# Four-layer convolution chain: the coarse wavelet sums of layer 1 as float32 products in 32-column strips

## The chip, the core and the metric

The kernel runs on one core of a Trainium2 chip. The metric is device time in microseconds (us) for one execution of the whole program, lower is better. Five engines work side by side and meet at semaphores: TensorE (PE in the profile, its weight loads PEld), VectorE (DVE), ScalarE (ACT), GpSimd (POOL) and SyncE (SP), whose queue issues the DMAs.

## The reference, cut to what matters

Four layers in a row work on `x` of 32 x 96 x 56 x 56 (batch, channels, rows, columns), each as `x = x + layer(_gn(x))`, where `_gn` is a normalisation over groups of three channels. Layer 0 is an expanding block with a depthwise convolution, layer 2 a quantised one, layer 3 a depthwise 9 x 9 convolution. The change is in layer 1, a wavelet convolution over three levels, for each channel by itself:

```python
def haar2d(x):
    a = x[:, :, 0::2, 0::2]; b = x[:, :, 0::2, 1::2]
    c = x[:, :, 1::2, 0::2]; d = x[:, :, 1::2, 1::2]
    ll = (a + b + c + d) * 0.5
    lh = (a - b + c - d) * 0.5
    hl = (a + b - c - d) * 0.5
    hh = (a - b - c + d) * 0.5
    return jnp.stack([ll, lh, hl, hh], axis=2)

cur = x
for i in range(3):
    co = haar2d(cur)
    cur = co[:, :, 0]                       # the sums go on to the next level
    flat = dwconv(co.reshape(B, C * 4, h, w), wconv_w[i]) * wscale[i]    # 5 x 5, depthwise
    level_coeffs.append(flat.reshape(B, C, 4, h, w))
next_ll = zeros
for i in reversed(range(3)):
    next_ll = ihaar2d(level_coeffs[i].at[:, :, 0].add(next_ll))
return dwconv(x, base_w) * base_scale + base_b + next_ll
```

So the first level works on 56 x 56, the second on the 28 x 28 sums of two by two points, the third on the 14 x 14 sums of those. What comes back from the third is added into the second, and that into the first.

## The kernel before

**Layout.** An image row of 56 is split into four column phases of 14 (`NPH`, `W4`). A channel's image is held in two halves `h` of 28 rows. One half lies in a tile with 112 partitions (28 rows x 4 phases) and 16 more for the halo of neighbouring rows, and 14 x 32 = 448 columns (column group, batch). Convolutions over rows and phases are then matrix products over the partitions, and steps between column groups are shifted views of the columns.

**Layer 1.** It goes over 48 pairs of channels. `load(i)` issues a pair's DMAs on SP: `images` (X, L736 and L739), `factors` (nr, L782), `matrices` (the row matrices of the first level, raw, L765 to L767; those of the second level, raw2, L838) and `third` (T3, L844). The steps are:

- `normal`: DVE scales and shifts X into x (L872, L873).
- `high` and `low`: ACT rounds x to float32r, a form that TensorE takes in one pass, into xh (L880); DVE writes the rest, x - xh, into xl (L884).
- `matrices1`, `matrices2`: ACT reorders raw and raw2 into T and T2 (L748, L775).
- `lowest1` (L897): the sums for the second level. Eight float32r products, for each half h, each parity n of the column group, and each of xh and xl, add up in one PSUM tile. Each (h, n) has its own 28 of the 112 output rows, and the other weights are zero. ACT copies the result to x2 (L900).
- `lowest2` (L906): the sums for the third level, two float32 products from x2; ACT copies them to x3 (L908).
- `level3` (L914), `level2` (L923, L924): the convolutions of the third and second level. ACT copies the third's output to c3 (L915, L916). The second's output is split into a rounded part and a rest, c2 (ACT L929, DVE L930).
- `level1`: `coarse` (L941) brings the second level up by float32r products, `fine` (L935) adds the first level by three float32 products, DVE adds the image (L954), and SP stores y (L961).

**Order.** PE, DVE, ACT and SP follow the program's order in this layer (`manual_schedule`). In one turn of the loop, pair i is in level1, pair i + 1 (`nxt`) in the sums and the upper levels, pair i + 2 (`far`) in normal and the matrices, and pair i + 3 is loaded. The turn begins with `load(i + 3)` and then:

```python
            do(lowest1, nxt)
            do(normal, far, 0, 0)
            do(matrices1, far, 0)
            do(normal, far, 0, 1)
            do(level1, i, 0, 0)
            do(lowest2, nxt)
```

Between the pairs, `left` gives out the last stores of layer 0 (L201), and `behind` prepares layer 2: its weights, and, every eighth pair, the first images that it will read (L1124). T2, T3, c2 and c3 are in three fixed sets of tiles, which POOL clears once at the start of the layer (L821). The first pair is prepared by `begin`.

**Names in the profile.** Numbers are left out of the names: the PSUM tiles pa1 and pa2 stand as pa, pc1 to pc3 as pc, x2 and x3 as x, T2 and T3 as T, c2 and c3 as c, raw2 as raw, y0 and y1 as y. In Layer 0, L426 is the expansion (full width), L449 and L493 are products that write strips of 32 columns, four of them next to each other.

Of the kernel before, what the change touches and what calls it, by code (L numbers as in the profile page):

```python
# [28 lines left out]
NPH = 4  # L29
# [599 lines left out]
NK = 3  # L629
# [128 lines left out]
LOW = 96  # L758

# [27 lines left out]
def layer1(ctx, tc, w, y0, left, made, norm, t1, t2, t3, y1, k2, behind):  # L787
# [18 lines left out]
    def rounded(name, shape):  # L806

        t = cp.tile(shape, F32R, tag=f"{name}r", name=f"{name}r")
        nc.scalar.copy(t, constant(name, shape))
        return t  # L810
# [3 lines left out]
    for i in reversed(range(NF)):  # L814
        sets[i] = {
            name: cp.tile(shape, dtype, tag=f"{name}{i}", name=f"{name}{i}") for name, shape, dtype in (
                ("T3", [128, 64 * KW], F32), ("T2", [PH, 2, NK, 128], F32), ("c2", [128, 2, 2, N2, B], F32R),
                ("c3", [128, N3, B], F32))}
# [4 lines left out]
    def load(i):  # L823

        st = {"i": i, **sets[i % NF], "X": [], "T": [None] * 2, "nr": [], "raw": [], "raw2": [], "pf": {}}
# [9 lines left out]
        def matrices(c):  # L835
            st["raw"].append(load_matrices(nc, pool, t1, c))
            raw = pool.tile([PH, NK * PH], F32, tag="raw2", name="raw2", bufs=4)
            nc.sync.dma_start(raw, t2[c])  # L838
            st["raw2"].append(raw)

        def third(c):
            at, n = c % 2 * HH, HH * KW
            for tile in range(2):
                nc.sync.dma_start(st["T3"][64 * tile + at : 64 * tile + at + HH, at * KW : at * KW + n], t3[c])  # L844
# [19 lines left out]
    def normal(st, j, h):  # L864

        if j + h == 0:
            st["x"] = pool.tile([128, 2, 2, W4, B], F32, tag="x", name="x", bufs=3)
            for n in ("xh", "xl"):
                st[n] = pool.tile([128, 2, 2, W4, B], F32R, tag=n, name=n, bufs=1)
# [5 lines left out]
    def parts(st, j):  # L875
        return (st[n][:, j].rearrange("p h q b -> p (h q b)") for n in ("x", "xh", "xl"))

    def high(st, j):
        x, xh, _ = parts(st, j)
        nc.scalar.copy(xh, x)  # L880

    def low(st, j):
        x, xh, xl = parts(st, j)
        nc.vector.tensor_tensor(xl, x, xh, ALU.subtract)  # L884

# [3 lines left out]
    def matrices2(st, j):  # L889
        ordered(nc, st["T2"][:, j], st["raw2"][j], 64)  # L890

    def lowest1(st):

        ps = psum.tile([128, 2, N2, B], F32, tag="w", name="pa1")
        parts = [(h, n, x) for h in range(2) for n in range(2) for x in ("xh", "xl")]
        for h, n, x in parts:
            nc.tensor.matmul(ps, low1[:, h, n, :], st[x][:, :, h, n::2, :],  # L897
                             start=((h, n, x) == parts[0]), stop=((h, n, x) == parts[-1]))
        st["x2"] = pool.tile([PH, 2, N2, B], F32, tag="x2", name="x2", bufs=2)
        nc.scalar.copy(st["x2"], ps[:PH])  # L900

    def lowest2(st):

        ps = psum.tile([128, N3, B], F32, tag="w", name="pa2")
        for j in range(2):
            nc.tensor.matmul(ps, low2[:, j, :], st["x2"][:, j], start=(j == 0), stop=(j == 1))  # L906
# [59 lines left out]
    def begin(st):  # L966
# [7 lines left out]
        for j in range(2):  # L974
# [4 lines left out]
            high(st, j)  # L979
        for j in range(2):  # L980
            low(st, j)
# [7 lines left out]
    with tc.manual_schedule(engines=MANUAL_SP):  # L989
        low1 = rounded("low1", [128, 2, 2, 128])  # L990
        up1 = rounded("up1", [128, 2, 2, 128])
        low2 = constant("low2", [PH, 2, 128])
        up2 = constant("up2", [128, 2, 128])
        pick = constant("pick", [C, 2, 128])
        for i in range(-3, PAIRS):
# [12 lines left out]
            do(high, far, 0)  # L1008
            do(low, far, 0)
# [6 lines left out]
            do(high, far, 1)  # L1016
# [4 lines left out]
            do(low, far, 1)  # L1021
# [551 lines left out]
def lowest_bands():  # L1573
# [24 lines left out]
    def twice(v, axis):  # L1598
        v = np.pad(v, [(0, 8 * (a == axis)) for a in range(v.ndim)])
        return np.concatenate([v, v], axis=axis)  # L1600

    return {"low1": low1, "low2": twice(low2, 2), "up1": up1, "up2": twice(up2, 0)}
# [115 lines left out]
```

## Time and profile before

| | us |
|---|---|
| median of 3 runs | 5655.76 (5650.31 to 5659.83) |
| the profiled execution | 5647.33 |
| its span, first to last instruction | 5645.5 |
| PE busy in the span | 5420.9 (96%) |
| DVE busy | 4691.7 (83%) |
| ACT busy | 4179.3 (74%) |
| POOL busy | 240.3 (4%) |

The 16 DMA engines together moved 456.13 MB in the span. The profile's page puts the span in 40 slices of 141 us; layer 1 lies in slices 20 to 25. A row of a group of instructions gives line, engine, operation, output and inputs, the form (weights' rows * columns, then partitions x columns), the count and the times. A row of the timeline gives start, length, engine, line and form; rows of the same kind that follow each other are merged, with their count at the end, and what is in brackets is the idle time before and what ended it. The end of a matmul is modelled and takes in the way through the array, so how often matmuls start tells what they cost.

### The profile page before, as it was taken

How to read it: one execution, taken by the hardware profiler on the slowest of the kernel's cores; microseconds unless marked ns; L12 is line 12 of the kernel's file. 1: busy time of each engine (PE TensorE's matmuls, PEld its weight loads, DVE VectorE, ACT ScalarE, POOL GpSimd, SP SyncE). 2: the span in 40 equal slices, each digit the busy share in tenths (PEclk: the TensorE clock that was granted, in tenths of full speed). 3: DMA queues.
4: the chain of work that ended last, by engine and by line, in shares of the span. 5: the costliest groups of instructions: out<-in, count | busy, mean ns of one | idle time of the engine just before them, and what ended most of it. 6: DMA issues, size and time to landing. Idle time of an engine off the chain costs nothing.

```text
span 5645.5 us, 137543 instructions
## 1 busy us (share of the span) xinstructions
PE 5420.9 (96%) x59704; PEld 3086.1 (55%) x59704; DVE 4691.7 (83%) x5413; ACT 4179.3 (74%) x6072; POOL 240.3 (4%) x161
## 2 busy tenths in 40 slices
PE   5999999999999999998899999999999999999999
PEld 2333333333333333333666666788878777787444
DVE  6999999999999999997777776777777777676777
ACT  5888888888888888885666664777777777676455
POOL 6000000000000000000000000000000000000000
PEclk9999999999999999998999999999999999999999
DMA  3023333322233232214577776479688697763888
GB/s 100 15 56 64 58 59 56 59 46 52 54 60 62 55 56 53 49 32 38 151 156 160 160 161 128 21 51 54 44 53 46 49 53 41 49 51 41 240 249 249
DMA packets 1289849, 456.13 MB, mean 81 GB/s; under 512 B 1104211, under 2 KB 1285187, under 8 KB 1287323
## 3 DMA queue, kind: packets, MB, share of 16 engines
q1 hardware_dynamic: 1289243, 447.32, 51.1%
q8 instruction: 469, 7.68, 0.6%
q14 instruction: 137, 1.12, 0.1%
HBM read 285.41 MB, written 214.08 MB: 88 GB/s over the span
## 4 chain that ended last, share of the span: by engine, by line
PE 82%; ACT 5%; DVE 5%; DMA 4%; issue 2%; SPq 1%; POOL 1%; ACTq 0%; DVEq 0%; POOLq 0%
PE psd L493 18%; PE psd L1294 13%; PE psj L548 11%; PE ps L426 8%; PE ps L1275 7%; PE pse L449 6%; PE pc L935 5%; PE pc L1469 4%; PE psj L1337 4%; DMA X<-y 2%; ACT hi L1245 2%; PE pc L923 1%; PE pa L897 1%; ACT u L1265 1%; DVE xl L884 1%
## 5 line engine op out<-in xcount | busy, mean ns | idle before, releaser
L467 DVE SCALAR_TENSOR_TENSOR h<-hpad,l_wdw,h 128x3136 f32<-128x3136 f32 x512 | 1782.2, 3481 | 9.1
L493 PE MATMUL psd<-plane,filt 128*32 128x392 f32 (+5 forms) x16384 | 1084.1, 485 | 0.6 <-issue 0.6
L1294 PE MATMUL psd<-apad,diag 64*64 64x392 bf16 x20736 | 914.5, 330 | 54.0 <-issue 50.1
L1294 PEld LDWEIGHTS <-diag 64*64 64x64 bf16 x20736 | 700.9, 106 | 262.8 <-issue 97.0
L493 PEld LDWEIGHTS psd<-plane,filt 128*32 128x32 f32 (+1 forms) x16384 | 389.5, 108 | 676.3 <-issue 623.5
L1265 ACT ACTIVATE u<-ps,o,s 128x784 int16<-128x784 f32 x576 | 537.4, 1003 | 164.9 <-PE ps L1275 145.9
L1265 ACT ACTIVATE a<-psd,o,s 128x784 int16<-128x784 f32 x448 | 424.6, 1002 | 263.3 <-PE psd L1294 263.2
L748 ACT COPY T<-raw 128x112 f32<-128x112 f32 (+2 forms) x1386 | 445.9, 385 | 230.0 <-DMA raw<-tdiff 170.3
L426 PE MATMUL ps<-xn,l_wboth 96*128 96x392 f32 (+1 forms) x1536 | 465.9, 506 | 23.9 <-ACT xn L408 23.2
L467 DVE SCALAR_TENSOR_TENSOR hc<-hhalf,l_wdw,hc 128x1568 f32<-128x1568 f32 x256 | 473.7, 1850 | 16.2 <-ACT hc L460 9.5
L1275 PE MATMUL ps<-hi,l_w1q 96*128 96x392 f32 x1280 | 464.0, 363 | 6.7 <-DVE u L1263 3.8
L935 PE MATMUL pc<-x,T 128*112 128x416 f32 (+1 forms) x1152 | 451.6, 529 | 6.1 <-DVE x L873 6.1
L1275 PE MATMUL ps<-lo,l_w1q 96*128 96x392 f32 x1280 | 439.2, 343 | 2.9 <-DVE lo L1253 2.9
L1469 PE MATMUL pc<-x,T 128*112 128x416 f32 (+1 forms) x1152 | 417.1, 523 | 13.8 <-ACT T L748 7.7
L449 PE MATMUL pse<-xn,l_wboth 96*32 96x392 f32 x4096 | 392.3, 501 | 4.5 <-ACT hab L470 4.5
L426 PEld LDWEIGHTS ps<-xn,l_wboth 96*128 96x128 f32 (+1 forms) x1536 | 219.4, 173 | 249.2 <-issue 54.5
L470 ACT ACTIVATE hab<-psd,o,s 128x784 f32<-128x784 f32 x256 | 283.7, 1113 | 59.5 <-PE psd L493 57.3
L1469 PEld LDWEIGHTS pc<-x,T 128*112 128x112 f32 x1152 | 203.2, 177 | 227.2 <-issue 188.7
L436 ACT ACTIVATE hpad<-ps,o,s 128x784 f32<-128x784 f32 x256 | 278.5, 1104 | 50.1 <-PE ps L426 48.8
L548 PE MATMUL psj<-h,wg 128*32 128x392 f32 x3072 | 306.4, 514 | 0.1
L548 PE MATMUL psj<-hab,wg 128*32 128x392 f32 x3072 | 304.8, 510 | 0.0
L935 PEld LDWEIGHTS pc<-x,T 128*112 128x112 f32 x1152 | 193.6, 180 | 154.9 <-issue 154.9
(267 smaller groups left out, 7684.8 us busy)
## 6 DMA issues: line engine op xcount, KB each, us to landing
X<-y SPq DMA_DIRECT2D x192, 392.0 KB
y<-xt SPq DMA_DIRECT2D x108, 392.0 KB
y<-y SPq DMA_DIRECT2D x96, 392.0 KB
out_dram<-y SPq DMA_DIRECT2D x96, 392.0 KB
twav<-zwav SPq DMA_DIRECT2D x768, 36.8 KB
y<-kept SPq DMA_DIRECT2D x72, 392.0 KB
xt<-y SPq DMA_DIRECT2D x59, 392.0 KB
xt<-in_x_dram SPq DMA_DIRECT2D x8, 2352.0 KB
```

The lines of the kernel that those rows point to most:

```text
L426: nc.tensor.matmul(ps[p, j, :NT], wexp[:, k * 128 : k * 128 + 128][:, m], im["xn"][:, j, rows, :].rearrange("c h w -> c (h w)"), start=Tru ...
L449: nc.tensor.matmul(ps[f * GC : (f + 1) * GC, half, :NT].rearrange("p (r w) -> p r w", w=W2), wexp[:, c : c + GC], im["xn"][:, f % 2, r0 : ...
L467: nc.vector.scalar_tensor_tensor(h2, taken(im, k, t), wdw[:, k, t : t + 1], h2, ALU.mult, ALU.add)
L470: nc.scalar.activation(view, ps, AF.Silu, bias=bi[1][:, c : c + 1], scale=sc[1][:, c : c + 1], accum_out=accum)
L493: nc.tensor.matmul(ps[at * GC : (at + 1) * GC, r, :NT].rearrange("p (r w) -> p r w", w=W2)[:, r0 - half * n : r1 - half * n, q0:q1], filt[ ...
L548: nc.tensor.matmul(ps[s * GC : (s + 1) * GC, t, :NT].rearrange("c (m r q) -> c r q m", m=2, q=W4), wg[p, k, c * GC : (c + 1) * GC], phases ...
L748: nc.scalar.copy(to.rearrange("x t (p s) -> x t p s", p=NPH), v[:, k])
L935: nc.tensor.matmul(ps[:PH, to], st["T"][j][:, h, k, :], st["x"][:, j, h, of], start=first and n == 0, stop=not first and n == NK - 1)
L1265: nc.scalar.activation(out, ps, AF.Identity, bias=o[:, c : c + 1], scale=s[:, c : c + 1])
L1275: nc.tensor.matmul(ps[:, j, :NT], w1[:, k * 128 : k * 128 + 128], im[part][:, r0 : r0 + RT, :].rearrange("c h w -> c (h w)"), start=(part ...
L1294: nc.tensor.matmul(ps[q, j, :NT].rearrange("p (r w) -> p r w", w=W), diag[p, k, t, :], v, start=(t == 0), stop=(t == 8))
L1469: nc.tensor.matmul(ps[:, :, to], st["T"][:, h, k, :], st["x"][:, h, :, of], start=(n == 0), stop=(n == NK - 1))
```

## The change

`lowest1` no longer reads high and low parts. Each (h, n) becomes one float32 product of x itself with a weight of 32 columns, 28 of them used, and writes its own strip of 32 PSUM partitions; nothing is added up. `high`, `low`, xh and xl go. x2 then has 128 partitions in four strips of 28 + 4. `lowest2` likewise makes four float32 products into four strips, two channels twice over, from one weight low2 of 128 x 32. To fit x2's partitions, T2 and raw2 are laid out in strips as well: raw2 becomes part of the fixed sets, is cleared by POOL, and is loaded by four DMAs for each pair of channels, in the second channel's turn, instead of one DMA for each channel. T3's blocks lie 32 instead of 28 apart. The constants low1, low2, up1 and up2 are built to match on the host.

```diff
+GC = 32
-                ("T3", [128, 64 * KW], F32), ("T2", [PH, 2, NK, 128], F32), ("c2", [128, 2, 2, N2, B], F32R),
+                ("T3", [128, 64 * KW], F32), ("T2", [128, 2, NK, 128], F32), ("raw2", [128, 2, NK * PH], F32), ("c2", [128, 2, 2, N2, B], F32R),
...
         def matrices(c):
             st["raw"].append(load_matrices(nc, pool, t1, c))
-            raw = pool.tile([PH, NK * PH], F32, tag="raw2", name="raw2", bufs=4)
-            nc.sync.dma_start(raw, t2[c])
-            st["raw2"].append(raw)
+            if c % 2:
+                for s in range(NPH):
+                    nc.sync.dma_start(st["raw2"][s * GC : s * GC + HH],
+                                      t2[c - 1 : c + 1, s * HH : (s + 1) * HH].rearrange("c x y -> x c y"))
 
         def third(c):
-            at, n = c % 2 * HH, HH * KW
+            at, n = c % 2 * GC, HH * KW
...
-    def high(st, j):
-        x, xh, _ = parts(st, j)
-        nc.scalar.copy(xh, x)
-
-    def low(st, j):
-        x, xh, xl = parts(st, j)
-        nc.vector.tensor_tensor(xl, x, xh, ALU.subtract)
...
     def matrices2(st, j):
-        ordered(nc, st["T2"][:, j], st["raw2"][j], 64)
+        ordered(nc, st["T2"][:, j], st["raw2"][:, j], 64)
 
     def lowest1(st):
 
         ps = psum.tile([128, 2, N2, B], F32, tag="w", name="pa1")
-        parts = [(h, n, x) for h in range(2) for n in range(2) for x in ("xh", "xl")]
-        for h, n, x in parts:
-            nc.tensor.matmul(ps, low1[:, h, n, :], st[x][:, :, h, n::2, :],
-                             start=((h, n, x) == parts[0]), stop=((h, n, x) == parts[-1]))
-        st["x2"] = pool.tile([PH, 2, N2, B], F32, tag="x2", name="x2", bufs=2)
-        nc.scalar.copy(st["x2"], ps[:PH])
+        for h in range(2):
+            for n in range(2):
+                strip = slice((2 * h + n) * GC, (2 * h + n + 1) * GC)
+                nc.tensor.matmul(ps[strip], low1[:, h, n, :], st["x"][:, :, h, n::2, :], start=True, stop=True)
+        st["x2"] = pool.tile([128, 2, N2, B], F32, tag="x2", name="x2", bufs=2)
+        nc.scalar.copy(st["x2"], ps)
 
     def lowest2(st):
 
         ps = psum.tile([128, N3, B], F32, tag="w", name="pa2")
-        for j in range(2):
-            nc.tensor.matmul(ps, low2[:, j, :], st["x2"][:, j], start=(j == 0), stop=(j == 1))
+        for strip in range(NPH):
+            nc.tensor.matmul(ps[strip * GC : (strip + 1) * GC], low2, st["x2"][:, strip % 2], start=True, stop=True)
...
-        low1 = rounded("low1", [128, 2, 2, 128])
+        low1 = constant("low1", [128, 2, 2, GC])
-        low2 = constant("low2", [PH, 2, 128])
+        low2 = constant("low2", [128, GC])
...
-            do(high, far, 0)
-            do(low, far, 0)
...
-            do(high, far, 1)
...
-            do(low, far, 1)
```

More of the change, by code (lines that the diff above doesn't have):

```diff
@@ L823, in load @@
     def load(i):
-        st = {"i": i, **sets[i % NF], "X": [], "T": [None] * 2, "nr": [], "raw": [], "raw2": [], "pf": {}}
+        st = {"i": i, **sets[i % NF], "X": [], "T": [None] * 2, "nr": [], "raw": [], "pf": {}}
         def images(c):
@@ L867, in normal @@
             st["x"] = pool.tile([128, 2, 2, W4, B], F32, tag="x", name="x", bufs=3)
-            for n in ("xh", "xl"):
-                st[n] = pool.tile([128, 2, 2, W4, B], F32R, tag=n, name=n, bufs=1)
         v, X, nr = st["x"][:, j, h], st["X"][j], st["nr"][j]
@@ L873, in normal @@
         nc.vector.tensor_tensor(v, v, bias, ALU.add)
-    def parts(st, j):
-        return (st[n][:, j].rearrange("p h q b -> p (h q b)") for n in ("x", "xh", "xl"))
-    def high(st, j):
-        x, xh, _ = parts(st, j)
-        nc.scalar.copy(xh, x)
-    def low(st, j):
-        x, xh, xl = parts(st, j)
-        nc.vector.tensor_tensor(xl, x, xh, ALU.subtract)
     def matrices1(st, j):
@@ L978, in begin @@
                 fine(st, j, h, True)
-            high(st, j)
-        for j in range(2):
-            low(st, j)
     sts = {}
@@ L1596, in lowest_bands, with strips @@
         up2[:, :, 64 * i : 64 * i + n] = low2[n * i : n * i + n].transpose(2, 1, 0)
[L1598 to L1602, printed above, removed]
+    def strips(v, axis):
+        shape = v.shape[:axis] + (-1, HH) + v.shape[axis + 1 :]
+        v = np.pad(v.reshape(shape), [(0, 4 * (a == axis + 1)) for a in range(v.ndim + 1)])
+        return v.reshape(v.shape[:axis] + (-1,) + v.shape[axis + 2 :])
+    of = [[low1[:, h, n, HH * (2 * h + n) : HH * (2 * h + n + 1)] for n in range(2)] for h in range(2)]
+    low1 = strips(np.array(of).transpose(2, 0, 1, 3), 3)
+    up2 = strips(up2, 0)
+    return {"low1": low1, "low2": strips(strips(low2[:, 0, :HH], 0), 1), "up1": up1, "up2": np.concatenate([up2, up2])}
 def layouts(a):
```

## The prediction

> **What bounds the kernel now.** I read the page first, then the windows of the second layer, then the waits there, then the order of time inside one pair of channels.
>
> ```profile
> span 5645.5 us, 137543 instructions
> PE 5420.9 (96%) x59704; PEld 3086.1 (55%) x59704; DVE 4691.7 (83%) x5413; ACT 4179.3 (74%) x6072; POOL 240.3 (4%) x161
> ```
>
> TensorE is busy nearly throughout, but a busy PE here may be waiting inside a modelled matmul, so the stage decides. Layer 1 runs from about 2677 to 3525 us, as 48 pairs of channels. The windows (busy time of PE, PEld, DVE, ACT, POOL, then granted clock, DMA share, GB/s), the last row one undisturbed pair:
>
> ```profile
> 3200.00:3300.00 100.00, 98.63 (x423) 66.57 (x423) 72.38 (x108) 65.25 (x182) 0.00 (x0) 1.00 0.72 146
> 3223.40:3239.93 16.53, 16.32 (x73) 11.07 (x71) 12.27 (x19) 10.85 (x31) 0.00 (x0) 1.00 0.58 162
> ```
>
> PE sets the pair's length; DVE has 4.3 us and ACT 5.7 us to spare. From the starts of the first sum product (L897) I get the 48 periods: about three quarters are 16.53 us within 0.02, the others are longer by 36 us together. Now one clean pair in order of time:
>
> ```profile
> 3239.65 1.09 DVE L884 TENSOR_TENSOR xl<-x,xh 128x896 fp32r<-128x896 f32 x1
> 3239.90 0.69 PE L897 MATMUL pa<-xh,low1r 128*128 128x448 f32 x1
> 3240.80 0.48 PE L897 MATMUL pa<-xl,low1r 128*128 128x448 f32 x1 [0.21 <-DVE xl L884]
> ...
> 3242.15 0.37 PE L897 MATMUL pa<-xl,low1r 128*128 128x448 f32 x1
> 3242.36 0.38 PE L941 MATMUL pc<-c,up1r 128*128 128x224 f32 x2
> 3242.57 2.31 PE L935 MATMUL pc<-x,T 128*112 128x448 f32 x6
> 3244.72 0.92 PE L906 MATMUL pa<-x,low 112*128 112x224 f32 x4
> 3245.32 0.54 PE L941 MATMUL pc<-c,up1r 128*128 128x224 f32 x2
> 3245.70 2.31 PE L935 MATMUL pc<-x,T 128*112 128x448 f32 x6
> 3247.93 1.24 PE L914 MATMUL pc<-x,T 64*64 64x224 f32 x10
> ```
>
> Starts count, not durations. Six records of L935 take 2.15 us (3242.57 to 3244.72). One float32 product is two records here (192 records of L906 are 96 products): 448 columns stream in 0.375 us a record, 224 columns in 0.187. A rounded product is one record: the L897 starts lie 0.207 apart. The first L897 starts about 0.33 before the L935 ahead of it is through (same offset at every pair), so the array is free for the sums at 3240.23 and goes on to L941 at 3242.36: **the first sum costs 2.13 us a pair**. Of that 8 x 0.207 = 1.66 is products and 0.47 is the wait for xl, which DVE finishes only at 3240.74. The second sum (L906) costs 4 x 0.187 and a little, 0.77.
>
> **The change, part by part.**
>
> *First sum.* Eight rounded products become four float32 ones, each into its own 32 columns. Nothing in Layer 1 is of that form, but Layer 0 has it:
>
> ```profile
> 907.08 1.52 PE L449 MATMUL pse<-xn,l_wboth 96*32 96x392 f32 x16
> 908.42 0.84 PE L493 MATMUL psd<-plane,filt 128*32 128x392 f32 x8
> ```
>
> Sixteen records of 392 columns, each 0.327 of streaming, take 1.34 us to the next line: not 5.2. They start in four waves of four, 7 ns apart in a wave, 0.309 to 0.333 between waves. L449 issues its strips one after another with one product each, as the change does, and L493 does so with 128 rows. So here: two waves of 0.375, plus 0.02 for the starts.
>
> Here a rule speaks against the change. The Trainium skill's page "FP8 and Floating Point Precision", section "TensorE Precision Notes", says true float32 takes four passes through the array. The trace agrees on the price of one product: 2 x 0.375 = 0.75 against 0.207 rounded. Taken alone it makes the sum 4 x 0.75 = 3.0 us, 0.9 dearer than now; by L449's row the four share one price, 0.77. I take the row, since it shows form and order both.
>
> Going in and out of strips costs something. "TensorEngine Tiling (Array Packing)", "Key Properties", says that a change of tiling mode drains TensorE, without a figure. The trace has one: L935 to the 64-column L914 takes 2.23 (3245.70 to 3247.93) against 2.15 to L906; the records give 93 ns there, 93 from L914 back to L941, and 95 from Layer 0's L426 into the strips of L449 and from them back. If the drain were a whole matmul's tail (an L449 record lasts 0.492 where it streams 0.327, so 0.165), the four switches of a pair would cost 0.28 more, 13 us in all; I take 0.095 and keep the other for the range.
>
> First sum after: 0.095 + 0.375 + 0.02 + 0.375 + 0.095 = 0.96. Saved: 2.13 - 0.96 = **1.17 us**. The xl wait goes with it, since x was written in the pair before. What is late next: the following L941 needs the c parts of DVE L930; they end 0.3 us before the sums now (3239.62), those of the half that is used first some 2 us earlier, so nothing waits even with the sum shorter.
>
> *Second sum.* 0.77 becomes 0.095 + 0.187 + 0.02 + 0.187 + 0.095 = 0.585; saved **0.18**. It needs ACT's copy x2, which ends 0.9 us after the sum while L941 and L935 run 2.4.
>
> *high and low.* Two ACT casts of 0.94 and two DVE subtractions of 1.09 leave each pair. DVE and ACT are not the bound, so beyond the xl wait they count nothing; DVE has about 10.1 and ACT 9.0 us of work in the new 15.2.
>
> *Same prices.* x2's copy writes 128 instead of 112 partitions, T2's copies and level2's products likewise: the cost follows columns (L748 takes 0.38 in all its row counts). The cast of low1 (0.60, at 2642) goes; ACT stood idle until 2670 anyway. Nothing for either.
>
> *raw2's loads.* Two issues of 147 KB a pair become four of 74 KB, all in the odd channel, behind raw's wait for ACT. Same bytes and same 1344-byte rows; two more issues of 0.42 on SP. SP issues about 10 us a pair now and 10.9 after, of 15.2; behind them stand T3's loads, the stores of y and the next images, all a pair or more ahead of need. raw2 itself now comes some 14 us into a pair and lands near 17; matrices2 wants it near 20 (15.2 plus 4.8). That 3 us, with 2 more until PE asks for c3, is the cover; were it gone, each us late would be a us of PE.
>
> *Start of the layer.* raw2 becomes a fixed tile, cleared on POOL. The first load of it must wait for that, and SP is in order:
>
> ```profile
> 2659.74 0.30 SPq L838 DMA_DIRECT2D raw<-twav  x1
> 2660.15 4.03 SPq L201 DMA_DIRECT2D y<-kept  x4
> 2669.79 1.04 POOL L821 MEMSET T<- 128x320 f32 x2
> 2671.99 0.32 SPq L736 DMA_DIRECT2D X<-y  x1
> 2677.40 11.38 PE L935 MATMUL pc<-x,T 128*112 128x448 f32 x24 [6.15 <-DVE x L873]
> ```
>
> POOL's memsets start at 2669.79, after Layer 0's last norm. T3 and T2 take 1.0, raw2 (672 columns, between 320 in 0.30 and 768 in 0.68) 0.6: SP gets on at about 2671.4. Four loads of 0.45, then the four stores y<-kept, which went at 2660 before: to 2675.2. The last one's traffic ended 2.9 us after its issue before, so the images come at about 2678.1 instead of 2672.0. **Cost: 6 us**, once, in full on the path, since PE waits for exactly these images. Bounds: 0 if POOL is given the memset earlier; 10 if the four loads of tdiff that stand there now (2670.1 to 2671.8) and slower landings add up. Tiles also move in memory and may wait for other tiles of Layer 0: inside these bounds.
>
> *The long pairs.* Their 36 us come from loads that are late. The worst follow the loads for Layer 2:
>
> ```profile
> 3000.22 4.24 SPq L1124 DMA_DIRECT2D xt<-y  x1
> 3004.50 7.17 SPq L736 DMA_DIRECT2D X<-y  x1
> ```
>
> SP is held for 12 us and the next two pairs lose 6. After the change the same delay meets pairs 1.35 shorter and a later raw2 (worse), but lowest1 no longer waits for ACT's cast behind the late T copies (better). Followed through one such stretch, I get 5 instead of 6; I count 0, with -15 to +30 over the layer for the range.
>
> **Sum.** 48 x (1.17 + 0.18) = 65 less, 6 more: 59 us. The profiled execution took 5647.33 us (span 5645.5), which makes it 5588; it lies 8 us under the median 5655.76, and against that median I forecast **5597 us**.
>
> **The rivals.** *The strips do not share the array* and run one after another: 8 records of 0.375 and 8 of 0.187 with four switches make 4.88 a pair against 2.90 now, +95, with the start +101: 5757 us, slower. It decides from 4.3 record times instead of the two I count. L449 and L493 speak against it; only the 448-column strided operand is new. Chance 0.05.
>
> *Supply becomes the bound*: SP and the DMA queue, with raw2 last, starve ACT after each block. For it: SP already waits for ACT (L765 on T, 64 us), the DMA share is 0.72. Against it: 0.58 in a clean pair. Price 4 to 8 us in each of five stretches, 20 to 40: about 5627. Chance 0.13.
>
> *The products were never the limit*, and the start eats what is left: the xl wait is replaced by another of the same length in each pair (c parts, x2): 48 x 0.5 less saved, and the start 10 instead of 6: 5625; still faster. Chance 0.05. Main line: 0.77.
>
> **How the numbers follow.** 5597; low end: no start cost and 15 less stall, 5576; high end: start 10, stalls +30, 5631, which takes in the second and third cases' middles. About 0.2% (11 us) is what a measurement here can tell from no change. Slower takes the strips' 0.05 and a tail of supply; same gets 0.03; faster 0.89.
>
> **What would show it.** Right: clean periods near 15.2; the four products' eight records in two waves; no wait on xl; first image load near 2678. Wrong: waves of one or two strips, switches well over 0.1, ACT waiting for raw2 in ordinary pairs, PE waiting for c or x2.

## The result, and the profile after

The changed kernel takes 5630.86 us (median of 20 runs, 5619.94 to 5653.11) against 5654.35 us for the kernel before (20 runs, 5642.26 to 5666.64): ratio 0.9963, with a 95% interval of 0.9954 to 0.9972. That is 16 to 26 us less by the ratio. It is faster, as forecast, but by less than half of the forecast 59 us.

The head of the page (span; then busy time, share and instructions of each engine):

```profile
span 5632.8 us, 138021 instructions
PE 5379.4 (96%) x59896; PEld 2975.1 (53%) x59896; DVE 4589.1 (81%) x5317; ACT 4096.6 (73%) x5975; POOL 242.4 (4%) x164
```

PE is 41.5 us less busy and the profiled span only 12.7 us shorter. The order of time in a clean pair, PE only:

```profile
3138.65 0.54 PE L930 MATMUL pc<-c,up1r 128*128 128x224 f32 x2
3139.02 2.31 PE L924 MATMUL pc<-x,T 128*112 128x448 f32 x6
3141.26 0.96 PE L887 MATMUL pa<-x,low 128*32 128x448 f32 x8
3142.15 0.48 PE L930 MATMUL pc<-c,up1r 128*128 128x224 f32 x2
3142.48 2.31 PE L924 MATMUL pc<-x,T 128*112 128x448 f32 x6
3144.72 0.58 PE L895 MATMUL pa<-x,low 128*32 128x224 f32 x8
3145.23 0.48 PE L930 MATMUL pc<-c,up1r 128*128 128x224 f32 x2
```

L887 is now the first sum and L895 the second, L924 the fine and L930 the coarse products. The eight records of L887 need 0.89 us to the next line, so the four strips share the array. The windows of one clean pair and of two late ones (busy time of PE, PEld, DVE, ACT, POOL, then granted clock, DMA share, GB/s):

```profile
3218.45:3233.89 15.44, 15.44 (x75) 9.03 (x74) 10.07 (x16) 9.15 (x28) 0.00 (x0) 1.00 0.63 169
2905.93:2929.15 23.22, 18.43 (x76) 10.27 (x75) 10.16 (x16) 8.82 (x28) 0.00 (x0) 0.85 0.80 151
2990.90:3015.77 24.87, 17.16 (x76) 9.83 (x75) 9.77 (x16) 8.23 (x26) 0.00 (x0) 0.86 1.00 145
```

In the clean pair PE has no gap left, and DVE and ACT have 5.4 and 6.3 us to spare. In the two late ones DVE and ACT do no more work than in the clean one, and the DMA share is higher.

The start of the layer, a few rows of its order of time:

```profile
2669.71 0.66 POOL L822 MEMSET raw<- 128x672 f32 x1
2670.39 1.62 SPq L840 DMA_DIRECT2D raw<-twav  x4
2672.11 3.17 SPq L201 DMA_DIRECT2D y<-kept  x4
...
2680.12 0.32 SPq L736 DMA_DIRECT2D X<-y  x1
```

SP stands at raw2's first loads (L840) until POOL has cleared raw2. The stores of Layer 0 (L201) leave at 2672.1 where they left at 2660.2, and the first image load follows at 2680.1 instead of 2672.0.

Where the time went, as the mean of two profiles each (the one shown and one more, in the next section). The parts are cut at the first and last product of the first sum and at the first products of Layers 2 and 3:

| us | before | after | difference | forecast |
|---|---|---|---|---|
| start to the first sum | 2687.5 | 2695.7 | +8.2 | +6 |
| 47 periods at the clean length | 777.2 | 725.7 | -51.5 | -63.5 |
| what the periods differ from that | 25.5 | 35.3 | +9.8 | 0 |
| last sum to Layer 2 | 37.1 | 36.2 | -0.9 | -1.4 |
| Layer 2 | 1687.2 | 1702.9 | +15.7 | 0 |
| Layer 3 to the end | 429.8 | 432.3 | +2.5 | 0 |

The differences add up to -16.2, and the spans differ by -16.1. Five questions follow from it: the start, the clean pair, the late pairs, Layer 2, and what a better version would be.

### The profile page after: what moved, and what is told of

Its sections match the earlier page's. It is cut to its first block, busy times and chain, and to the rows that moved or that the text cites. A ratio compares the mean times of both kernels' runs of the same rounds, so it can differ in the third digit from the quotient of the medians.

```text
span 5632.8 us, 138021 instructions
## 1 busy us (share of the span) xinstructions
PE 5379.4 (96%) x59896; PEld 2975.1 (53%) x59896; DVE 4589.1 (81%) x5317; ACT 4096.6 (73%) x5975; POOL 242.4 (4%) x164
## 4 chain that ended last, share of the span: by engine, by line
PE 78%; DMA 6%; ACT 5%; DVE 4%; SPq 3%; issue 2%; POOL 1%; ACTq 0%; DVEq 0%; POOLq 0%
PE psd L493 18%; PE psd L1276 13%; PE psj L548 11%; PE ps L426 8%; PE ps L1257 7%; PE pse L449 6%; PE pc L924 5%; PE psj L1319 4%; DMA X<-y 4%; ACT hi L1227 2%; PE pc L1451 2%; ACT u L1247 1%; PE pc L912 1%; DVE h L467 1%; ACT a L1247 1%
## 5 line engine op out<-in xcount | busy, mean ns | idle before, releaser
L1276 PEld LDWEIGHTS <-diag 64*64 64x64 bf16 x20736 | 688.4, 106 | 298.1 <-issue 121.2
L748 ACT COPY T<-raw 128x112 f32<-128x112 f32 (+1 forms) x1386 | 445.9, 385 | 326.3 <-DMA raw<-tdiff 179.9
L467 DVE SCALAR_TENSOR_TENSOR hc<-hhalf,l_wdw,hc 128x1568 f32<-128x1568 f32 x256 | 473.7, 1850 | 16.2 <-ACT hc L460 9.5
L924 PE MATMUL pc<-x,T 128*112 128x416 f32 (+1 forms) x1152 | 451.3, 529 | 15.3 <-DVE x L873 15.3
L449 PE MATMUL pse<-xn,l_wboth 96*32 96x392 f32 x4096 | 391.0, 500 | 3.2 <-ACT hab L470 3.2
L436 ACT ACTIVATE hpad<-ps,o,s 128x784 f32<-128x784 f32 x256 | 278.3, 1103 | 49.6 <-PE ps L426 48.0
L924 PEld LDWEIGHTS pc<-x,T 128*112 128x112 f32 x1152 | 193.6, 180 | 163.6 <-issue 163.6
```

The costliest lines, as they stand in the source:

```text
L449: nc.tensor.matmul(ps[f * GC : (f + 1) * GC, half, :NT].rearrange("p (r w) -> p r w", w=W2), wexp[:, c : c + GC], im["xn"][:, f % 2, r0 : ...
L467: nc.vector.scalar_tensor_tensor(h2, taken(im, k, t), wdw[:, k, t : t + 1], h2, ALU.mult, ALU.add)
L748: nc.scalar.copy(to.rearrange("x t (p s) -> x t p s", p=NPH), v[:, k])
L924: nc.tensor.matmul(ps[:PH, to], st["T"][j][:, h, k, :], st["x"][:, j, h, of], start=first and n == 0, stop=not first and n == NK - 1)
L1276: nc.tensor.matmul(ps[q, j, :NT].rearrange("p (r w) -> p r w", w=W), diag[p, k, t, :], v, start=(t == 0), stop=(t == 8))
```

## The experiments

"Excess" below is the sum, over the 47 periods of Layer 1, of what each is longer than the clean period. The third row of the table also counts the first two periods, which are shorter than a clean one, by 5 us together before and 8 after. Times and ratios are against the kernel before on the same chip.

**The same kernels again** (no edit).

> The kernel before, unchanged, to see how much Layer 2 differs from one execution to the next. In the first profiles Layer 1 got 41 us shorter, but Layer 2 (first product of its expansion to the first product of Layer 3) got 25 us longer, 1682 to 1707, though its instructions are the same: TensorE stood still for more than 0.9 us between two of its products 42 times before (58 us together) and 60 times after (85 us), each time a whole number of 256 instructions apart. Theory A (chance: these stops vary from execution to execution): Layer 2 here may be anything from 1680 to 1710. Theory B (the changed program itself has more of them, because its stream of instructions or its transfers meet differently): Layer 2 here is within 8 us of 1682, with about 42 stops.

Measured: 5644.61 us; clean period 16.53; excess 24.5, against 36.3 in the profile that the prediction read; Layer 2 1692.6 against 1681.8.

> The changed kernel once more. Layer 1 should repeat within 5 us (pairs at 15.44, first coarse sum at 2697, last fine product at 3483). Layer 2: theory A (chance) allows 1680 to 1710; theory B (the program) gives 1707 within 8 us and about 60 stops.

Measured: 5625.25 us; clean period 15.44; excess 44.6 against 41.7; Layer 2 1698.7 against 1707.1. So, as far as two profiles of each kernel can tell, the clean period is certain to 0.01 us, an excess to some 6 us and a single length of Layer 2 to some 5 us.

### The start: late_start

```diff
-            if c % 2:
-                for s in range(NPH):
...
+            if c % 2 and c > 1:
+                second(c)
...
+        def second(c):
+            for s in range(NPH):
...
             for c in range(2):
                 third(c)
+            second(1)
             return st
```

`second` holds the same four loads. The first pair's come after its images, and `begin` calls matrices2 after its fine products.

> For the first pair only, raw2 is loaded last, after the images, the norm and T3, and ACT's matrices2 for it come after the normalising. Theory of the prediction: the first images waited on SP behind raw2's loads, which waited for POOL's memset: the first coarse sum starts at 2688 to 2690 as before the change instead of 2697, 7 to 9 us less in all. Rival: moved tiles wait for Layer 0's memory: it stays at 2696 to 2698.

Measured: 5621.39 us, ratio 0.9942 (0.9926 to 0.9959). Its start, in order of time:

```profile
2660.17 3.26 SPq L201 DMA_DIRECT2D y<-kept  x4
...
2670.89 0.32 SPq L736 DMA_DIRECT2D X<-y  x1
2676.21 11.38 PE L928 MATMUL pc<-x,T 128*112 128x448 f32 x24 [6.06 <-DVE x L877]
```

The stores are back at 2660.2, the first image load at 2670.9 and the first sum at 2687.5, as before the change. So the 8 us come from raw2's first loads, which stand in front of the queue and wait for POOL.

### The clean pair: fine_first

The change saves 1.09 us a pair, not 1.35. In the records, going into strips costs 94 ns, as forecast. Coming out costs 94 ns, and then the first product of the next line is followed late: the second L930 starts 0.208 us after the first, where two of them otherwise lie 0.105 apart. The question is whether that time belongs to L930, so that another product could hide it, or to the way out of the strips.

```diff
-            coarse(st, j, h, True)
-            fine(st, j, h, False)
+            fine(st, j, h, True)
+            coarse(st, j, h, False)
```

> level1 issues its three fine products before its two coarse ones. A clean pair went from 16.53 to 15.44 us and not to the predicted 15.19. In the records the two coarse products that come out of a strip stand 0.208 apart instead of 0.105. Theory: the weights of the second one are loaded in the open there, 0.10 for each of three exits a pair (after both coarse sums and after level3), and a long fine product behind the exit would hide that: 15.14 a pair, about 14 us less over the layer. Rival: the 0.10 belongs to the change of mode and whatever comes first pays it: 15.44 stays.

Measured: 5621.02 us, ratio 0.9948 (0.9932 to 0.9963); clean period 15.37. The order of time of a pair:

```profile
3138.44 0.96 PE L887 MATMUL pa<-x,low 128*32 128x448 f32 x8
3139.33 2.40 PE L924 MATMUL pc<-x,T 128*112 128x448 f32 x6
3141.25 0.69 PE L930 MATMUL pc<-c,up1r 128*112 128x224 f32 x2
3141.87 0.59 PE L895 MATMUL pa<-x,low 128*32 128x224 f32 x8
```

L887 again takes 0.89 to the next line. Now the first L924 record is followed after 0.467 instead of 0.375 us: whichever product comes first out of the strips pays about 0.09 to 0.1. That is the expectation's rival, nearly: the new order wins back 0.07 us a pair, 3 us in all, and not 0.3. The kernel before already shows this price behind its own 64-column product:

```profile
3247.93 1.24 PE L914 MATMUL pc<-x,T 64*64 64x224 f32 x10
3249.11 0.48 PE L941 MATMUL pc<-c,up1r 128*128 128x224 f32 x2
3249.42 2.31 PE L935 MATMUL pc<-x,T 128*112 128x448 f32 x6
```

From L941 to L935 it takes 0.31 here, and 0.21 in the pair of the prediction (3242.36 to 3242.57), where full-width products came before. (The 0.38 behind L906, from 3245.32 to 3245.70, is no counterexample: the first L941 record only starts early there, 28 ns after the last of L906. From L906's start to L935 it takes 0.98 us, which is four records of 0.19 and the same 0.21.)

### The late pairs: who makes them late

**raw2_even** issues raw2's four loads in the pair's first channel instead of its second, so that they come earlier:

```diff
-            if c % 2:
+            if c % 2 == 0:
...
-                                      t2[c - 1 : c + 1, s * HH : (s + 1) * HH].rearrange("c x y -> x c y"))
+                                      t2[c : c + 2, s * HH : (s + 1) * HH].rearrange("c x y -> x c y"))
```

> The changed kernel with the four loads of raw2 in the first channel's turn instead of the second's. The pairs that are late cost 42 and 45 us over 47 periods in the changed kernel, 36 and 25 in the kernel before; the longest follow the loads for Layer 2. If raw2's late place is what starves ACT there (the rival of the prediction), the late pairs fall to 25 to 35 us. If it is the first-level raw, held behind the blocked queue and met by shorter pairs, they stay at 40 to 47.

Measured: 5640.03 us in one run; excess 38.7, against 41.7 and 44.6. That is within what an excess scatters: no effect of raw2's place is seen.

**x3_first** puts ACT's copies of the first-level matrices behind the copy to x3, for which PE waits in a late pair:

```diff
-            do(matrices1, far, 0)
             do(normal, far, 0, 1)
             do(level1, i, 0, 0)
             do(lowest2, nxt)
+            do(matrices1, far, 0)
```

> The changed kernel with matrices1 of the first channel moved behind lowest2, so that ACT copies x3 before it waits for raw. In the late pairs of the changed kernel level3 waits up to 8 us for ACT's x3, which stands behind a T copy that waits for raw. If that queue order is what hands the late load on to TensorE, the late pairs fall from 42 to 45 us to 20 to 30, at the same 15.44 for the clean ones. If the load is late for everything that follows as well, they stay within 5 us.

Measured: 5640.15 us in one run; excess 51.5. The other order does not help: ACT still waits for the same data, and the copies that were put later are later still.

**split_loads** cuts each of the ten early loads for Layer 2 in two by channels, and issues one piece a pair:

```diff
-            for i, pair in enumerate(self.pairs):
-                self.nc.sync.dma_start(pair[g * GR : (g + 1) * GR], self.y1[g][:, :, 2 * i : 2 * i + 2, :])
+            self.pieces += [(g, n, i) for i in range(2) for n in range(2)]
...
+        for g, n, i in self.pieces[:1]:
+            k = GR // 2
+            self.nc.sync.dma_start(self.pairs[i][g * GR + n * k : g * GR + (n + 1) * k],
+                                   self.y1[g][n * k : (n + 1) * k, :, 2 * i : 2 * i + 2, :])
+        del self.pieces[:1]
```

> The changed kernel with Layer 2's early image loads in pieces: instead of two loads of 392 KB together every eighth pair (SP then stands for some 12 us), four of 196 KB, one after each of four pairs. Theory: late pairs are the loads of Layer 1 held up behind that block, and they grew from about 31 us (three profiles with the old sums) to 43 (five with the new) because the same block meets shorter pairs: in pieces they fall to 15 to 28 us, the whole 15 to 25 us faster than the changed kernel. Rival: the volume of small packets is what delays, however it is issued: 38 to 48 us, spread over more pairs.

Measured: 5671.82 us, ratio 1.0039 (1.0021 to 1.0056), slower than before; excess 87.5. So these loads matter, but these pieces made it worse. Two questions were open: are these loads the source of the whole difference, and what is wrong with the pieces?

**before_loads_at_end and loads_at_end** issue all ten loads after Layer 1, in the two kernels:

```diff
-                    k2.begin(min(2 * pair, C - GR))
+                    k2.begin(C - GR if pair == PAIRS - 1 else 0)
```

> The kernel before, with the ten big loads that Layer 2 needs early (kept and xt) all issued after Layer 1's last pair instead of during it, so that Layer 2 starts late (an estimate of 20 to 45 us; its start is not what is read here). Theory (the late pairs come from these loads): the excess of the late pairs in Layer 1 falls from the 25 to 36 us of the three profiles of before to under 15. Rival (the excess comes from the layer's ordinary traffic): it stays at 20 or more.

> The changed kernel with the same edit. If the growth of the late pairs by the change (from 31 to 43 us on average) is what the early loads cost more when pairs are shorter, the excess here lies within 4 us of that in the kernel before with the loads at the end. If it is a growth of its own (raw2's place, SP's extra issues), the excess here stays 8 us or more above it.

Measured: excess 12.3 in the kernel before and 5.5 in the changed one (5684.31 and 5643.55 us; both pay for it at Layer 2). The early loads cost the kernel before 12 to 24 us (excess 24.5 and 36.3, less 12.3), and the changed one 36 to 39.

What is left of the excess before, 12.3, lies in the first eight periods, and so do 10.5 us of the excess in each of the two profiles of the unchanged kernel. There PE waits for xl, which is behind late casts (first row) or behind DVE's work for the weights of Layer 2 (second row):

```profile
2720.38 0.74 PE L897 MATMUL pa<-xl,low1r 128*128 128x448 f32 x1 [2.37 <-DVE xl L884]
...
2809.07 0.74 PE L897 MATMUL pa<-xl,low1r 128*128 128x448 f32 x1 [3.32 <-DVE xl L884]
```

After the change the same eight periods have 0.3 us of excess. So the +9.8 of the table is the sum of a gain and a greater loss: the first eight periods became 13 us shorter against the clean length (the first two, which are short, give 3 of it), and the other 39 became 23 us longer.

Here is how the early loads make a pair late, in the chain of work through one late pair of the changed kernel (start, length, what):

```profile
2894.61 1.89 SPq L1106
...
2896.55 5.77 SPq L1106
...
2902.36 5.59 SPq L736
...
2909.93 4.50 DMA raw<-twav
...
2914.46 0.97 ACT T L748 x3
...
2916.92 0.36 ACT x L897
...
2917.32 2.19 PE pc L903 x9
```

The two early loads (L1106) and the image load behind them hold SP for 13 us. The matrices of the pair are issued only then and land at 2914.4; ACT waits 7.0 us for them, its copy to x3 stands behind, and PE waits for x3. ACT's wait for these loads between 2830 and 3370 us, before (first line) and after (second; total, times, longest):

```profile
ACT T L748 <- DMA raw<-twav: 11.7, 6, 3.1
...
ACT T L748 <- DMA raw<-twav: 67.0, 21, 9.9
```

And PE's waits for xl and x3 between 2830 and 3480 us, before (two lines) and after (one line; the second profiles have 17.2, 0.7 and 30.9):

```profile
PE pa L897 <- DVE xl L884: 16.7, 37, 3.3
PE pc L914 <- ACT x L908: 4.1, 3, 2.5
...
PE pc L903 <- ACT x L897: 25.3, 8, 7.7
```

Before the change PE stops at xl; after it, at x3. SP also has less time to make up for a burst. Between 2830 and 3370 us all its waits for others, its slack, add up to 119 and 112 us in the two profiles before and to 62 and 69 after. Those for ACT's copies to T, before and after:

```profile
SPq L765 <- ACT T L748: 43.9, 40, 1.6
...
SPq L766 <- ACT T L748: 16.6, 20, 2.1
```

The slack is thus about 3.6 us a pair before and 2.0 after. The pairs are 1.09 us shorter, and SP has two more issues in each, which the prediction put at 0.9 us. No run takes these two apart.

**split_rows** cuts the loads into as many pieces as split_loads did, but each has all 16 channels and half of the rows:

```diff
+            k = H * NPH // 2
+            self.nc.sync.dma_start(self.pairs[i][g * GR : (g + 1) * GR, n * k : (n + 1) * k],
+                                   self.y1[g][:, n * k : (n + 1) * k, 2 * i : 2 * i + 2, :])
```

> Each early load in two pieces, one a pair of channels as in the split by channels (excess 87.5 us), but each piece has all 16 channels and half of the rows. Theory (a piece that spans half of the partitions takes as long as a whole load, so that split by channels doubled the traffic time): excess 35 to 50, as without the split. Rival (any split doubles the number of disturbed pairs, whatever its shape): 75 or more.

Measured: 5604.06 us in one run; excess 26.9. That is 60 less than the split by channels with the same bytes and the same count, and lower than either theory had it. The semaphore events of the landings, which the trace keeps one by one, point to why (medians from the issue, us):

| early load | KB | events | last one lands |
|---|---|---|---|
| whole, 16 channels | 392 | 16 | 10.8 (kept), 16.0 (xt behind it) |
| half the channels, 8 | 196 | 9 | 10.4 |
| half the rows, 16 channels | 196 | 16 | 7.1 to 7.4 |

Half the channels take as long as the whole: 9 events, one of them about 1 us after the issue. The Trainium skill's page "DMA: Bandwidth & Descriptors", section "Why a DMA increments its semaphore by 16 and not by 1", has the rule: a DMA spreads over the largest number of engines, up to 16, that divides the slowest dimension of both sides, and the issuing sequencer writes the semaphore at once for the engines that are not used. By that rule 8 channels use 8 engines and 16 channels use 16. The events agree.

**spread** issues the loads whole, kept and xt in successive pairs of channels:

```diff
+            self.pieces += [(g, i) for i in range(2)]
...
+        for g, i in self.pieces[:1]:
+            self.nc.sync.dma_start(self.pairs[i][g * GR : (g + 1) * GR], self.y1[g][:, :, 2 * i : 2 * i + 2, :])
+        del self.pieces[:1]
```

> The early loads whole, but the two of a group (kept, then xt) in successive pairs of channels instead of one right behind the other. If SP held for 12 us in one pair is what makes pairs late, the excess falls to 20 to 32 us and the kernel is 10 to 20 us faster than the changed one (about 5612 us). If each load costs what it costs wherever it stands, the excess stays at 38 to 50 and the time near 5630. If two disturbed pairs in a row cost more than one, it grows to 50 to 90, as with the split by channels.

Measured: 5625.35 us, ratio 0.9961 (0.9944 to 0.9979); excess 39.3, as in the changed kernel. Keeping whole loads apart does not help in this profile.

**before_split_rows** is the edit of split_rows in the kernel before.

> The kernel before with the early loads of Layer 2 in pieces of half the rows, as in split_rows. With the loads moved to the end its excess was 12.3 us, so of its 25 to 36 us some 19 belong to these loads; by the changed kernel (37 of them became 21) about 8 to 11 of the 19 go: excess 17 to 26, and 5635 to 5645 us. If the mended loads help only where the pairs are short, excess 28 or more and no change of the time.

Measured: 5646.83 us, ratio 0.9981 (0.9969 to 0.9993); excess 11.4, less than expected, and no more than with the loads at the end. One pair with such a piece, in the kernel before (before_split_rows) and in the changed one (split_rows) (windows, columns as above):

```profile
2924.68:2941.22 16.54, 16.34 (x73) 11.07 (x71) 12.28 (x19) 10.86 (x31) 0.00 (x0) 1.00 0.78 156
...
2936.11:2954.41 18.30, 15.78 (x76) 9.02 (x75) 9.60 (x15) 8.64 (x27) 0.00 (x0) 1.00 0.66 154
```

In a 16.53 us pair the twenty pieces cost PE nothing. In a 15.44 us pair some still do: this one takes 18.30. The excess of 11.4 is again that of the first eight periods, but for 0.9 us.

### Layer 2, whose code is the same

The stops of PE there lie in the depthwise products, and they come at whole numbers of instructions. A stretch of the order of time after the change (in brackets the idle time before; each product has a weight load, so 128 products are 256 instructions):

```profile
3620.22 8.39 PE L1276 MATMUL psd<-apad,diag 64*64 64x392 bf16 x183
3629.99 11.28 PE L1276 MATMUL psd<-apad,diag 64*64 64x392 bf16 x256 [1.38 <-issue]
3642.97 5.63 PE L1276 MATMUL psd<-apad,diag 64*64 64x392 bf16 x128 [1.70 <-issue]
3649.45 3.74 PE L1276 MATMUL psd<-apad,diag 64*64 64x392 bf16 x81 [0.85 <-issue]
```

Counted through the program, every stop within these products falls on the same number modulo 256 (193 or 194), in both kernels. The Trainium skill's page "Runtime: NRT & Kernel Launch", section "Instruction fetch mechanics", says that instructions are fetched in blocks of 256 and that crossing a block is mostly hidden. The 256 agrees; hidden it is not. Distances over 0.9 us between the starts of two depthwise products add up to 57 and 64 us in the two profiles of before, and to 85 and 76 after.

The fetch itself is in the trace, in a DMA queue of its own. The changed kernel from 3493 to 5200 us, Layer 2 (packets, MB, share of 16 engines):

```profile
q8 instruction: 194, 3.18, 1.0%
```

These are packets of 16 KB, one for every 255 instructions of PE and its weight loads (49,521 in the layer). Each of the 56 stops of this profile ends 1.2 to 2.1 us after one of these packets has ended, and the later the packet, the longer the stop (correlation 0.93). So the stops are waits for instructions. Which products a block's end hits depends on how many PE instructions came before: Layer 2 starts at 185 modulo 256 before the change, and at 149 after.

**after_pad9 and before_pad55** add small products ahead of Layer 1, so that each kernel gets (nearly) the other's number, 184 and 148. Nine of them, and 55 of the same kind in the kernel before:

```diff
+        pp = psum.tile([128, 2, 2 * B + 1], F32, tag="w", name="pp0")
+        for _ in range(9):
+            nc.tensor.matmul(pp[:GC, 0, :1], low1[:, 0, 0, :GC], low2[:, :1], start=True, stop=True)
```

> The changed kernel with nine one-column float32 products more in begin, where TensorE waits for the first images; their result is not used. They are 36 instructions, so that in Layer 2 every 256th instruction falls on the same products of an image as in the kernel before (its Layer 2 starts at instruction 185 of a block of 256, the changed kernel's at 149). In four profiles of the changed program and its variants Layer 2 takes 1699 to 1707 us, in two of the kernel before 1682 and 1693; image 8 takes 56 against 50, image 30 takes 54 against 49.5, each time. Theory: the stops are waits for the next block of 256 instructions, and where a block ends inside an image decides how many there are: Layer 2 goes to 1680 to 1695, image 8 to about 50 and image 30 to 49.5, the whole is 12 to 17 us faster than the changed kernel. Rival: something else in Layer 2 (transfers that start earlier, tiles in other places) makes the stops: it stays at 1699 to 1707, with images 8 and 30 as in the changed kernel.

Measured: 5631.22 us, ratio 0.9952 (0.9935 to 0.9969); Layer 2 1697.3.

> The kernel before with 55 one-column float32 products more in begin (220 instructions, result not used), which puts its Layer 2 where the changed kernel's stands in the blocks of 256. Theory (block ends): Layer 2 rises from 1682 to 1693 to 1699 to 1707, images 8 and 30 to 56 and 54 us, 12 to 17 us slower in all than the kernel before. Rival: it stays at 1682 to 1693, and the whole within 5 us.

Measured: 5659.4 us, ratio 1.0017 (1.0004 to 1.0030); Layer 2 1698.5. Two of the 32 images follow the number in all twenty profiles. Images 6 and 30, counted from 0, take 49.4 to 49.6 us each (from their first expansion product to the next image's) in every profile with 182 to 185 (four of the kernel before, and both padded kernels with the change), and 52.6 to 57.2 in every other one, before_pad55 among them. That is about 10 us for the two. But other images went the other way, and the layer as a whole hardly follows: without no_fetch, Layer 2 took 1682 to 1707 with 182 to 185 (six profiles, mean 1693), and 1678 to 1713 with the others (thirteen, mean 1698). In the times, the padding cost the kernel before 10 us by the ratio (2 to 17 by the interval). It won the changed kernel some 6, with intervals that overlap, and best, below, nothing. So how much of the 15.7 belongs to this number stays open.

**no_fetch** leaves out Layer 2's image loads from the seventh image on.

```diff
-            if b >= 2 * len(k2.pairs):
+            if 2 * len(k2.pairs) <= b < 2 * len(pairs):
```

> The changed kernel without Layer 2's own loads of images from the seventh on: each image pair then works on what its tile holds, so these values are not the layer's; the instructions of PE, DVE and ACT are the same. It asks what makes TensorE stop at every 256th instruction in Layer 2. Theory: the next block of instructions comes by DMA and waits behind the layer's image transfers, so with about half of them gone the stops fall from 49 to 60 (76 to 85 us) to under 30 (40 us) and Layer 2 from 1699 to 1707 to below 1670. Rival: a block's fetch is slow by itself: 45 to 60 stops as before.

Measured: 5600.35 us in one run; Layer 2 1671.3. The stops over 0.9 us fall from 56 to 32, and from 84.8 to 53.7 us, against the first profile of the changed kernel (46 and 75.5 in the second). So about a third of the time of the stops goes with the image loads that run beside the fetch; the expectation had half. When these loads fall is a second thing that moves with everything ahead of Layer 2.

### The version that beats both

**best** is late_start, fine_first and split_loads together, with the pieces by channels. **best_pad9** adds the nine products of after_pad9.

> Late start, fine products first and split loads together, on the changed kernel. If the parts add up: 8 to 10 us at the start, 3 in the clean pairs, 15 to 25 in the late pairs: 5595 to 5605 us, 0.8 to 1.0% under the kernel before. If late pairs are only moved: 5612 to 5622.

> The same with nine one-column products more at the start (36 instructions, result not used), which moves the block ends in Layer 2 to where they stand in the kernel before. If that is worth in time what it was in one profile: 5 to 10 us less than without; if block ends shift with the rest of the program and even out: the same within 5 us.

Measured: 5664.2 us, ratio 1.0019 (1.0004 to 1.0034), and 5666.81 us, ratio 1.0024 (1.0010 to 1.0038); excess 97.4 in the first. The start was mended (first sum at 2688.3 and 2687.3), but the pieces by channels took far more than all of it.

**best_rows** is late_start, fine_first and split_rows.

> The changed kernel with raw2's first loads after the images (late_start), the fine products in front of the coarse ones (fine_first) and the early loads in pieces of half the rows (split_rows). If the three gains add: start 9 us, 0.07 us in each of 48 pairs (3), late pairs 14 to 16: 5601 to 5609 us, ratio to the kernel before 0.990 to 0.993. Rival (the single profile of split_rows was a lucky one: its kernel with the loads in successive pairs also had one run at 5601 beside others near 5627): 5613 to 5622, ratio 0.994 to 0.9955. If forecast and kernel differ only by what these three mend and by Layer 2, it stays 48 to 52 us below before_split_rows plus its own gain of late pairs, that is, near 44 below it.

Measured: 5610.41 us (6 runs, 5595.89 to 5615.47), ratio 0.9910 (0.9894 to 0.9927): the best of all, 51 us under the kernel before by the ratio and 46 by the medians. Clean period 15.37, first sum at 2687.7, but excess 38.8: its pairs are shorter than those of split_rows (26.9), and the pieces of the first two groups still make them late (22 us), as do the last three periods (14.5). Against before_split_rows it is 36 us less by the medians and 40 by the ratios; expected were 44.

## Why the prediction was right or wrong

What the change does to the sums was forecast rightly; the total was not. The forecast was 59 us, the medians give 23.5 and the profiles 16. Three terms were wrong: the clean pair was mis-sized (12.5 us with the last pair), the long pairs were put at 0 (9.8), and the layers behind Layer 1 had no term (18.2). The start gives 2.2, and this makes up the 43 us that the profiles miss.

- **Strips share the array: right.** Eight records in two waves, 0.89 us to the next line where 0.865 was forecast. The reading of L449's row held, and four passes for each product alone, the rule that spoke against it, did not decide.
- **The wait for xl is gone: right.** No wait on x in a clean pair; DVE 10.07 and ACT 9.15 us of work against the forecast 10.1 and 9.0.
- **The clean pair: mechanism right, a term mis-sized.** 1.09 us saved of 1.35; 15.44, not 15.19. The switch out of strips was costed at 0.095; it is 0.095 and about 0.1 more on the product that follows. Two switches out a pair make 0.2 of the 0.26. The row that shows it (L941 behind L914) stood in the trace of before. Price: 12 to 13 us.
- **The start: right in mechanism, near in size.** Forecast 6, image load at 2678.1; measured 8.2, load at 2680.1. The bounds 0 to 10 held it.
- **The long pairs: this step failed.** "I get 5 instead of 6; I count 0": in the stretch that the prediction followed, a loss of 6.3 became 9.4 and, in the second profile, 13.6. It let lowest1's freedom from ACT's cast cancel the shorter pairs. That wait did go: 16.7 us for xl from 2830 us on, of which some 0.2 falls to every clean pair. But ACT's copy to x3 stands behind the same late T copies, and PE's wait for x3 grew from 4.1 to 25.3 us (0.7 to 30.9 in the second profiles). What ends last now is the matrices' load behind SP's 13 us, then ACT and x3, and no cast of x stands in that chain. The early loads alone cost 36 to 39 us instead of 12 to 24.
- **Its range of -15 to +30 held the net 9.8, in part by luck.** Two misses stood against each other: 23 us more behind the first eight periods, and 13 us less in them, where work that the change took away had been in PE's way. The prediction put all 36 us of the long pairs down to late loads; some 6 of them, in the seventh and eighth period, stand beside DVE's work for the weights of Layer 2 instead. That the median of 5630.86 lies just inside the range up to 5631 is luck too, since the range had no room for Layer 2.
- **The rival "supply becomes the bound" was right in part.** It priced 20 to 40 us more in five stretches behind the early loads. By the means, these loads cost 18 us before and 38 after, 20 more, and the loss of SP's slack fits it. But it named raw2 as what starves ACT; the chain has the first-level matrices instead, and raw2_even saw no effect of raw2's place.
- **Layer 2 was not in the forecast.** It grew by 15.7 us in two profiles each. Its stops are waits for instructions, and in two images 10 us follow the place of the 256-instruction blocks. As whole layers the two places differ by 4 us in the mean, less than single profiles scatter. So the cause of the 15.7 as a whole stays open, as does that of Layer 3's 2.5.

## What to carry to other kernels

Cost a switch of TensorE's tile shape by the starts of the first two products behind it, not only by the gap in front. When one engine's stage is made shorter, check each burst of transfers in it against the shorter stage: what stands behind the burst in the same queue, which engine passes the delay on, and how much slack the issuing queue keeps to catch up. Cut a large load along an inner dimension, so that the outer one still spreads it over all DMA engines. Work that is taken off an engine with time to spare can still be worth something where that engine is busy for another stage. And a change to the number of instructions ahead of a later, untouched stage can move single stretches of it, so leave room for that in a forecast.

## What was not expected of the hardware

- A DMA that spans 8 channels left 9 landing events and took 10.4 us for 196 KB; one that spans 16 left 16 and took 10.8 us for 392 KB. By the same reading, raw2's new loads of 28 rows use fewer engines (15 events) than the old one of 112 rows (16): they carry half the bytes and take 2.4 us where it took 2.5, both by the median.
- A late pair costs more than PE's wait. In the pair of 23.22 us shown above, PE waits 4.8 us, and right behind the wait the granted clock is 0.50 for 6.7 us (third row, a window as above), so that products take nearly twice as long:

```profile
2917.32 2.19 PE L903 MATMUL pc<-x,T 64*64 64x224 f32 x10 [4.79 <-ACT x L897]
...
2919.99 4.04 PE L924 MATMUL pc<-x,T 128*112 128x448 f32 x6
...
2916.70:2923.40 6.70, 6.08 (x17) 3.44 (x18) 4.94 (x8) 2.55 (x10) 0.00 (x0) 0.50 0.54 125
```

L924 takes 2.31 otherwise. Over the pair PE works 18.43 us at a mean clock of 0.85, where the same products take 15.44 us at 1.00: 3.0 of the 7.8 us lost are the clock. The kernel before has the same: 22.03 us, with a mean clock of 0.85 and PE busy for 19.21 instead of 16.32.
- The first product after a narrow one holds up its successor by about 0.1 us, on top of the 94 ns gap in front of it.
- At the end of a block of 256 PE instructions PE can stand idle for up to 5.0 us in a stretch of short products (kernel before, second profile), more so while image loads run.
